# A two-layer graph network on one core: TensorE's work for three chunks set side by side, in written order

## The chip, the core and the metric

The kernel runs on one core of a Trainium2 chip. The core has five engines with a queue of instructions each: TensorE (PE; its weight loads are listed apart as PEld), VectorE (DVE), ScalarE (ACT), GpSimd (POOL) and SyncE (SP). DMA queues move data between HBM and the on-chip memories; those that fetch rows by a list of indices are issued by POOL, plain ones by SP and ACT. The metric is the time of one execution in device microseconds (us); the median of four runs is 15922.23 us (15918.34 to 15925.62).

## The reference

There are 50000 nodes with 128 features, and 850000 edges (src, dst, rel), sorted by dst, with one of 16 relations each. Two layers of this kind run one after the other, and the result is added to x and normalized:

```python
def _rgcn_layer(h, src, dst, rel, basis, w_comp, loop_w, bias):
    W = jnp.einsum('rb,bio->rio', w_comp, basis)          # 16 relations from 8 bases
    seg = dst.astype(jnp.int32) * N_REL + rel.astype(jnp.int32)
    agg = jax.ops.segment_sum(h[src], seg, num_segments=N_ENT * N_REL)
    agg = agg.reshape(N_ENT, N_REL, -1)
    msg = jnp.einsum('nri,rio->no', agg, W)
    out = msg + h @ loop_w + bias
    return jax.nn.relu(out)
...
x = _layernorm(x + layer2(layer1(x)), axis=-1)
```

## The kernel before, in words

**Chunks.** The edges are cut into runs of 672, two runs to a chunk: C = 633 chunks, the last with one run. Edges from a node to itself are taken out of the runs beforehand and handled apart ("node tiles", below), which leaves at most 640 edges a run: 5 rows of 128 (`HALF`), 10 a chunk (`K`). The function `runs(g, ...)` prepares a group of 128 runs (64 chunks): it closes up the runs on DVE (`closed_up`, six steps), turns source indices and destination keys on PE (`put`, L382 to 389; transposes at L388), writes the relations to HBM (REL), computes each run's place among the nodes (`slot`, L410 to 436), and collects the edges from a node to itself (`loops_of`, ten more steps of `closed_up`), whose relations go to LREL in HBM by one scatter of POOL per group (L491, ten in all). It is a generator; in layer one, each chunk takes one step of it for the next group (L688 to 692), beginning with the third chunk of a group. Group 0 is prepared before and during chunk 0.

**A chunk's work, in the order in which it is written.**

1. Ten gathers on POOL (L697, recorded as L187): each fetches 128 rows of h, one per edge, into one tenth of a buffer `g`. Six such buffers take turns (`GATHERS`), so a gather writes where the chunk six before it was read.
2. For every fourth chunk `weights` (L544): loads relations, compares them on DVE (`is_rel`), and five products on PE (L556) give each edge its eight basis weights in PSUM (`pm`). DVE makes `hot` (L711): for each edge, eight weights spread over 12 places for the destination nodes.
3. **Products with A** (L722): ten products g x hot in two halves of five, each half copied by ACT into `aT` (L729). A float32 product is recorded as two matmuls.
4. After the first half, `finish` for the chunk before: **products with bases** (`slots`, L619: eight products over the bases, summed in PSUM, copied by ACT), then **products with nodes** (L634 places the sums at their nodes, L638 adds what the chunk before carried over), the sum with the own part `L` (L640), and the store of 128 nodes to H1 (L647), or in layer two `normed` and the store to the output (L651).
5. Also after the first half, `from_itself` for as many node tiles of 128 nodes as are due (391 tiles over 633 chunks, six of them at chunks 0 and 1): load `h_own`, transpose on PE (L194), two products with four bases each (L599) into one PSUM buffer `hb`, weighted by DVE (L602), the loop product (L609), a sum on DVE (L612) and the store to `L`. For every eighth tile `loop_weights` (L565) loads LREL and makes the weights of the edges from a node to itself with two products (L582).
6. The loads for `finish`: `ls_of` from L and, in layer two, `xw` from x.

**What sets the order.** The program is traced in that order, and the framework's planner then orders each engine's queue by its own estimate of when things are ready; on the chip each engine runs its queue strictly in the planned order and waits on semaphores. So PE's order above is the planner's, and it may take the work of several chunks in turn. Gathers of layer two read H1 and wait for all of it. `count_up` (L499), traced in the last chunk of layer one, has one small product and tells whether the preparation held; if not, a slow path runs, which doesn't happen here.

Of the kernel before, what the change touches and what calls it, by code (L numbers as in the profile page):

```python
# [38 lines left out]
F32 = mybir.dt.float32  # L39
# [36 lines left out]
def tile_rgcn_resnorm(  # L76
# [255 lines left out]
    def runs(g, pool, asked):  # L332
# [58 lines left out]
        put(srcf, src)  # L391
# [12 lines left out]
        put(keyf, key)  # L404
        rel8 = pool.tile([P, LIVE], U8, name="rel8")
        nc.scalar.copy(rel8, quarters[:, :LIVE, 3])
        nc.sync.dma_start(REL[r0 : r0 + P], rel8)
        yield
# [15 lines left out]
        nc.scalar.copy(offs, po[:HALF, :])  # L424
        po = ps_o.tile([P, D], F32, name="po")
# [102 lines left out]
    def chunked():  # L528
        with (
# [14 lines left out]
            def weights(c, n):  # L544

                rel = hp.tile([P, LIVE], U8, name="rel")
                nc.sync.dma_start(
                    rel,
                    bass.AP(tensor=REL.tensor, offset=REL.offset + 2 * c * LIVE, ap=[[LIVE, AT], [0, NR], [1, LIVE]]),
                )  # L550
                is_rel = hp.tile([P, LIVE], F32, name="is_rel")
                nc.vector.tensor_scalar(is_rel, rel, its_rel, None, op0=OP.is_equal)  # L552
                pm = ps_m.tile([P, AT * PER * NB], F32, name="pm")
                of = pm.rearrange("e (t j) -> e t j", t=AT)
                for j in range(PER):
                    nc.tensor.matmul(  # L556
                        of[:, :, j * NB : (j + 1) * NB],
                        is_rel[:, j * P : (j + 1) * P],
                        EACH[n],
                        start=True,  # L560
                        stop=True,
                    )
                return pm.rearrange("e (t b) -> e t b", b=NB)

            def loop_weights(i, n):  # L565
# [13 lines left out]
                nc.vector.tensor_scalar(is_rel[:m], rel[:m], its_rel1[:m], None, op0=OP.is_equal)  # L579
                po = ps_o.tile([P, D], F32, name="po")  # L580
# [6 lines left out]
                return lw  # L587

            def from_itself(i, of, lw, n):

                m = min(P, N - i * P)
                h = sb.tile([P, D], F32, name="h_own")
                nc.sync.dma_start(h[:m], of[i * P : i * P + m, :])
                hT = turned(h[:m], m, sb)
                by = sb.tile([P, NB + 1, D], F32, name="by", bufs=1)
                few = BANK // D
                for b in range(0, NB, few):
                    hb = ps_h.tile([P, BANK], F32, name="hb")
# [8 lines left out]
                    )  # L607
                po = ps_o.tile([P, D], F32, name="po")
# [4 lines left out]
                nc.sync.dma_start(L[n][i * P : i * P + m, :], ls[:m])  # L613

# [11 lines left out]
            def finish(kept, c, k, aT, n0, ls, xw, n):  # L626

                st = slots(c, k, aT, n)
# [51 lines left out]
            some = ()  # L680
            for n, of in enumerate((x, H1)):
                kept, late, looked, lw = None, None, 0, None
                for c in range(C):
# [9 lines left out]
                    ks = HALF * min(2, R - 2 * c)  # L693
                    n0 = at(c)
                    g = rows[(n * C + c) % GATHERS]
                    for k in range(ks):
                        gather(g[:, k, :], of, src[:, c * K + k : c * K + k + 1])  # L697
                    if n == 0 and c == 0:
                        done(first_runs)
                    if c % Q == 0:  # L700
                        pm = weights(c, n)
                    t0 = c % Q * K
                    own = hp.tile([P, K, WN], F32, name="own")
                    nc.vector.tensor_tensor(
                        own[:, :ks],
                        grid[:, None, :WN].to_broadcast([P, ks, WN]),
                        key[:, c * K : c * K + ks, None].to_broadcast([P, ks, WN]),
                        op=OP.is_equal,
                    )
                    hot = hp.tile([P, K, NB, WN], F32, name="hot")  # L710
                    nc.vector.tensor_tensor(  # L711
                        hot[:, :ks],
                        pm[:, t0 : t0 + ks, :, None].to_broadcast([P, ks, NB, WN]),
                        own[:, :ks, None, :].to_broadcast([P, ks, NB, WN]),
                        op=OP.mult,
                    )
                    aT = hp.tile([P, NB, S], F32, name="aT")
                    for k in range(0, ks, PER):
                        m = min(PER, ks - k)
# [13 lines left out]
                        if k == 0:  # L733
                            if late is not None:
                                kept = finish(kept, *late)
                            while looked < asked(c):
                                if looked % AT == 0:
                                    lw = loop_weights(looked, n)
                                from_itself(looked, of, lw[:, looked % AT, :], n)
                                looked += 1  # L740
                    ls = sb.tile([P, D], F32, name="ls_of")
                    nc.sync.dma_start(ls, L[n][ds(n0, P), :])
                    xw = None
                    if n:
                        xw = sb.tile([P, D], F32, name="xw")
                        nc.sync.dma_start(xw, x[ds(n0, P), :])
                    late = c, ks, aT, n0, ls, xw, n
# [4 lines left out]
                finish(kept, *late)  # L752
# [188 lines left out]
```

## Time and profile before

| | |
|---|---|
| median of four runs | 15922.23 us |
| the profiled execution's own time | 15926.42 us |
| its span | 15924.6 us |
| granted clock of TensorE, mean | 0.767 |
| POOL: gathers of layer one / two | 6007.5 us / 5983.5 us busy, 6325 each |
| PE: products with A (L722) | 5592.9 us busy, 25300 matmuls |
| PE: products with bases (L619) | 3785.8 us busy, 20256 matmuls |
| PE: products with nodes (L634, L638) | 605.4 and 547.7 us busy |

A line of the timeline reads: start, length, engine, line of the kernel, operation, what it writes <- what it reads, shape, count, and in brackets how long the engine had been idle before and what ended that. A line of the groups reads: line, engine, operation, tiles, shapes, count | busy us, mean ns of one | idle us of the engine before them and what ended most of it. Busy time leaves out the fixed step between two instructions of an engine, and the time in which a gather's rows travel.

### The profile page before, as it was taken

How to read it: one execution, taken by the hardware profiler on the slowest of the kernel's cores; microseconds unless marked ns; L12 is line 12 of the kernel's file. 1: busy time of each engine (PE TensorE's matmuls, PEld its weight loads, DVE VectorE, ACT ScalarE, POOL GpSimd, SP SyncE). 2: the span in 40 equal slices, each digit the busy share in tenths (PEclk: the TensorE clock that was granted, in tenths of full speed). 3: DMA queues.
4: the chain of work that ended last, by engine and by line, in shares of the span. 5: the costliest groups of instructions: out<-in, count | busy, mean ns of one | idle time of the engine just before them, and what ended most of it. 6: DMA issues, size and time to landing. Idle time of an engine off the chain costs nothing.

```text
span 15924.6 us, 190376 instructions
## 1 busy us (share of the span) xinstructions
PE 11711.7 (74%) x59828; PEld 9645.4 (61%) x59828; DVE 6491.1 (41%) x14282; ACT 2763.7 (17%) x7931; POOL 12005.3 (75%) x12673
## 2 busy tenths in 40 slices
PE   5767677777777676767777777777777777777777
PEld 4656565656656565656666666666666666666666
DVE  5434444343434343433344444444444444444443
ACT  1111111111111111111111111111111111111111
POOL 7777777777777777777777777777777777777777
PEclk8777777777777777777777777777777777777777
DMA  3222222222222222222222222222222222222222
GB/s 84 76 72 76 72 77 72 76 72 76 72 76 72 75 72 73 72 74 73 71 76 77 78 78 78 78 78 78 78 78 78 78 78 78 77 78 78 78 77 72
DMA packets 1169578, 1207.74 MB, mean 76 GB/s; under 512 B 285749, under 2 KB 960949, under 8 KB 1168560
## 3 DMA queue, kind: packets, MB, share of 16 engines
q0 software_dynamic: 405232, 830.17, 20.2%
q1 hardware_dynamic: 760112, 363.84, 8.0%
q8 instruction: 481, 7.88, 0.2%
q14 instruction: 537, 4.40, 0.1%
q10 hardware_dynamic: 3216, 1.45, 0.0%
HBM read 1058.61 MB, written 135.71 MB: 75 GB/s over the span
## 4 chain that ended last, share of the span: by engine, by line
PE 36%; DMA 34%; issue 18%; POOL 5%; DVE 1%; ACT 0%; POOLq 0%; SPq 0%; DVEq 0%; ACTq 0%
DMA g<-H,src 18%; DMA g<-in_x_dram,src 16%; PE ps L619 15%; PE pa L722 10%; PE hb L599 6%; POOL g L187 5%; PE pm L556 2%; PE pn L634 1%; PE pn L638 1%; PE po L609 1%; PE po L194 1%; PE po L582 0%; DVE ls L612 0%; DVE hot L711 0%; DMA lrel<-LREL 0%
## 5 line engine op out<-in xcount | busy, mean ns | idle before, releaser
L722 PE MATMUL pa<-hot,g 128*128 128x96 f32 x25300 | 5592.9, 337 | 3957.1 <-DMA g<-H,src 1905.8
L722 PEld LDWEIGHTS pa<-hot,g 128*128 128x128 f32 x25300 | 4331.0, 229 | 5390.2 <-DMA g<-H,src 2354.0
L187 POOL DMA_INDIRECT g<-in_x_dram,src x6325 | 6007.5, 950 | 1952.0 <-issue 1085.3
L187 POOL DMA_INDIRECT g<-H,src x6325 | 5983.5, 946 | 1943.9 <-issue 1082.4
L619 PE MATMUL ps<-basis,aT 128*120 128x128 f32 x20256 | 3785.8, 362 | 22.3 <-ACT aT L729 22.1
L619 PEld LDWEIGHTS ps<-basis,aT 128*120 128x120 f32 x20256 | 3605.6, 266 | 102.1 <-ACT aT L729 52.2
L729 ACT COPY aT<-pa 128x480 f32<-128x480 f32 x2530 | 1414.4, 559 | 9013.0 <-PE pa L722 9000.6
L602 DVE TENSOR_TENSOR by<-hb,lw 128x512 f32<-128x512 f32 x1564 | 1079.1, 690 | 3989.2 <-PE hb L599 3964.9
L711 DVE TENSOR_TENSOR hot<-pm,own 128x960 f32<-128x960 f32 x1266 | 1445.7, 1150 | 1616.8 <-PE pa L722 1002.9
L599 PE MATMUL hb<-basis,hT 128*128 128x512 f32 x3128 | 1827.4, 669 | 10.8 <-ACT hT L196 7.9
L612 DVE TENSOR_REDUCE ls<-by 128x128 f32<-128x1152 f32 (+1 forms) x782 | 1648.6, 2108 | 2.9
L630 DVE TENSOR_SCALAR own<-fixed,slot 120x128 f32<-120x128 f32 x1266 | 433.5, 342 | 1097.5 <-PE pn L634 1095.5
L623 ACT COPY slots<-ps 120x128 f32<-120x128 f32 x1266 | 337.8, 267 | 2436.6 <-PE ps L619 2434.5
L634 PE MATMUL pn<-slots,own 120*128 120x128 f32 x2532 | 605.4, 326 | 19.5 <-ACT slots L623 16.9
L640 DVE TENSOR_TENSOR a<-pn,ls_of 128x128 f32<-128x128 f32 x1266 | 358.5, 283 | 617.5 <-DMA ls_of<-L 192.9
L634 PEld LDWEIGHTS pn<-slots,own 120*128 120x128 f32 x2532 | 479.2, 226 | 207.4 <-issue 85.8
L599 PEld LDWEIGHTS hb<-basis,hT 128*128 128x128 f32 x3128 | 540.8, 216 | 17.2 <-ACT hT L196 12.7
L638 PE MATMUL pn<-kept,shift 128*128 128x128 f32 x2528 | 547.7, 302 | 0.0
L643 ACT COPY kept<-pn 128x128 f32<-128x128 f32 x1264 | 340.6, 269 | 1075.1 <-DVE a L640 1056.3
L556 PEld LDWEIGHTS pm<-each,is_rel 128*128 128x128 f32 x3180 | 450.4, 213 | 86.8 <-issue 77.8
L521 DVE RECIPROCAL rs<-sd 128x1 f32<-128x1 f32 x633 | 100.8, 159 | 941.5 <-ACT sd L519 938.6
L556 PE MATMUL pm<-each,is_rel 128*128 128x64 f32 x3180 | 455.6, 292 | 8.7 <-DVE is_rel L552 8.7
(142 smaller groups left out, 4989.2 us busy)
## 6 DMA issues: line engine op xcount, KB each, us to landing
g<-in_x_dram,src POOLq DMA_INDIRECT x6325
g<-H,src POOLq DMA_INDIRECT x6325
ls_of<-L SPq DMA_DIRECT2D x1266, 64.0 KB
L<-ls SPq DMA_DIRECT2D x780, 64.0 KB
H<-h SPq DMA_DIRECT2D x633, 64.0 KB
xw<-in_x_dram SPq DMA_DIRECT2D x633, 64.0 KB
out_dram<-o SPq DMA_DIRECT2D x633, 64.0 KB
rel<-REL SPq DMA_DIRECT2D x318, 80.0 KB
```

Source lines behind the costliest of these rows:

```text
L187: nc.gpsimd.indirect_dma_start(out=to, out_offset=None, in_=of, in_offset=bass.IndirectOffsetOnAxis(ap=idx, axis=0))
L556: nc.tensor.matmul(of[:, :, j * NB : (j + 1) * NB], is_rel[:, j * P : (j + 1) * P], EACH[n], start=True, stop=True,)
L599: nc.tensor.matmul(hb[:m], hT, BASIS[n][:, b : b + few, :].rearrange("p b d -> p (b d)"), start=True, stop=True)
L602: nc.vector.tensor_tensor(by[:m, b : b + few, :], hb[:m].rearrange("p (b d) -> p b d", d=D), lw[:m, b : b + few, None].to_broadcast([m, fe ...
L612: nc.vector.tensor_reduce(ls[:m], by[:m].rearrange("p b d -> p d b"), AX.X, OP.add)
L619: nc.tensor.matmul(ps[: k * WN], aT[:, b, : k * WN], BASIS[n][:, b, :], start=b == 0, stop=b == NB - 1)
L630: nc.vector.tensor_scalar(own[: k * WN], grid[: k * WN, :P], slot[: k * WN, c : c + 1], None, op0=OP.is_equal)
L634: nc.tensor.matmul(pn, own[: k * WN], st[: k * WN], start=True, stop=not c)
L638: nc.tensor.matmul(pn, shift, kept, start=False, stop=True)
L711: nc.vector.tensor_tensor(hot[:, :ks], pm[:, t0 : t0 + ks, :, None].to_broadcast([P, ks, NB, WN]), own[:, :ks, None, :].to_broadcast([P, k ...
L722: nc.tensor.matmul(pa[:, i * NB * WN : (i + 1) * NB * WN], g[:, k + i, :], hot[:, k + i].rearrange("e b w -> e (b w)"), start=True, stop=True,
L729: nc.scalar.copy(aT[:, :, k * WN : (k + m) * WN].rearrange("d b (i w) -> d i b w", w=WN), pa[:, : m * NB * WN].rearrange("d (i b w) -> d i ...
```

## The change

PE's instructions in the two layers are put under a manual schedule: PE's queue takes them exactly as they are traced. The other engines stay with the planner. The tracing is rearranged so that one iteration holds, for PE, in this order:

- nodes for chunk c-2 (`nodes_of`, the second part of the old `finish`);
- the weights and the transpose of the first node tile of this iteration;
- A, first half, for chunk c;
- that tile's first basis product, then bases for chunk c-1 (`slots`), then the tile's second basis product;
- A, second half, for chunk c;
- the rest of that tile (the loop product), and all further node tiles of this iteration, each from its beginning to its end;
- weights for the chunk after, if it is the first of four.

`weights`, `loop_weights` and `from_itself` become generators, so that their loads and DVE's comparisons are traced an iteration ahead of their products, and `hot` of the next chunk at the end of an iteration. The node tiles of chunks 0 and 1 all come at chunk 1. `ls_of` and `xw` are loaded an iteration after their chunk's A products, for nodes an iteration later. `runs` gets three more pauses; for all groups but the first the transposes of the source indices move behind one of them, so all later steps of a group, its scatter too, are traced two chunks later.

```diff
-        put(srcf, src)
+        if g == 0:
+            put(srcf, src)
...
-        put(keyf, key)
         rel8 = pool.tile([P, LIVE], U8, name="rel8")
         nc.scalar.copy(rel8, quarters[:, :LIVE, 3])
         nc.sync.dma_start(REL[r0 : r0 + P], rel8)
+        yield
+        if g:
+            put(srcf, src)
+        put(keyf, key)
         yield
...
         nc.scalar.copy(offs, po[:HALF, :])
+        yield
...
-            def from_itself(i, of, lw, n):
+            def from_itself(i, of, n, lws):
 
                 m = min(P, N - i * P)
+                if i % AT == 0:
+                    weigh = loop_weights(i, n)
+                    next(weigh)
                 h = sb.tile([P, D], F32, name="h_own")
                 nc.sync.dma_start(h[:m], of[i * P : i * P + m, :])
+                yield
+                if i % AT == 0:
+                    lws[:] = [next(weigh)]
+                lw = lws[0][:, i % AT, :]
                 hT = turned(h[:m], m, sb)
...
                 for b in range(0, NB, few):
+                    yield
                     hb = ps_h.tile([P, BANK], F32, name="hb")
...
+                yield
                 po = ps_o.tile([P, D], F32, name="po")
                 nc.tensor.matmul(po[:m], hT, LOOP[n], start=True, stop=True)
...
-            def finish(kept, c, k, aT, n0, ls, xw, n):
-
-                st = slots(c, k, aT, n)
+            def nodes_of(kept, c, k, st, n0, ls, xw, n):
+
...
+            ordered = ExitStack()
+            ordered.enter_context(tc.manual_schedule(engines={mybir.EngineType.PE}))
             for n, of in enumerate((x, H1)):
...
+                def own_nodes(c):
+
+                    return range(asked(c - 1) if c > 1 else 0, asked(c) if c else 0)
...
                 for c in range(C):
...
+                    if c == 0:
+                        if n == 0:
+                            done(first_runs)
+                        pm = next(weigh)
+                        hot = hot_of(c, pm)
+                    if c > 1:
+                        kept = nodes_of(kept, c - 2, ks(c - 2), summed_up, base[2], *others, n)
+                        others = loaded(base[1])
+                    parts = own_parts[0] if own_parts else iter(())
+                    next(parts, None)
...
                         if k == 0:
-                            if late is not None:
-                                kept = finish(kept, *late)
-                            while looked < asked(c):
-                                if looked % AT == 0:
-                                    lw = loop_weights(looked, n)
-                                from_itself(looked, of, lw[:, looked % AT, :], n)
-                                looked += 1
...
+                            next(parts, None)
+                            if c:
+                                summed_up = slots(c - 1, ks(c - 1), multiplied, n)
+                            next(parts, None)
+                    multiplied = aT
+                    for parts in own_parts:
+                        done(parts)
+                    if c == 1:
+                        others = loaded(base[1])
+                    if c + 1 < C:
+                        if (c + 1) % Q == 0:
+                            pm = next(weigh)
+                        hot = hot_of(c + 1, pm)
+                        if c + 2 < C and (c + 2) % Q == 0:
+                            weigh = weights(c + 2, n)
+                            next(weigh)
+                        own_parts = []
+                        for i in own_nodes(c + 1):
+                            own_parts.append(from_itself(i, of, n, lws))
+                            if len(own_parts) == 1:
+                                next(own_parts[0])
...
-                finish(kept, *late)
+                last = loaded(base[0])
+                kept = nodes_of(kept, C - 2, ks(C - 2), summed_up, base[1], *others, n)
+                summed_up = slots(C - 1, ks(C - 1), multiplied, n)
+                nodes_of(kept, C - 1, ks(C - 1), summed_up, base[0], *last, n)
+            ordered.close()
```

## The prediction

> **What bounds the kernel now.** I read the page's busy shares first, then its groups, then the waits of POOL alone, then stretches of PE, then the timeline around the two kinds of place where PE falls behind.
>
> ```profile
> PE 11711.7 (74%) x59828; PEld 9645.4 (61%) x59828; DVE 6491.1 (41%) x14282; ACT 2763.7 (17%) x7931; POOL 12005.3 (75%) x12673
> ...
> PE 36%; DMA 34%; issue 18%; POOL 5%; DVE 1%; ACT 0%; POOLq 0%; SPq 0%; DVEq 0%; ACTq 0%
> ...
> L187 POOL DMA_INDIRECT g<-in_x_dram,src x6325 | 6007.5, 950 | 1952.0 <-issue 1085.3
> L187 POOL DMA_INDIRECT g<-H,src x6325 | 5983.5, 946 | 1943.9 <-issue 1082.4
> ```
>
> POOL and PE look level (75% and 74%), and the chain runs mostly along PE and the gathers' landings. But POOL's gathers are 6007.5 + 5983.5 us busy and 1952.0 + 1943.9 us idle before them: 15886.9 of the 15924.6 us of the span. POOL's waits say what the idle time is (columns: total, times, longest, in us):
>
> ```profile
> POOL g L187 <- issue: 2167.7, 7112, 0.3
> POOL g L187 <- PE pa L722: 597.4, 1960, 0.3
> ...
> POOL g L187 <- ACT src L389: 24.6, 1, 24.6
> POOL g L187 <- DMA H<-h: 16.4, 1, 16.4
> ```
>
> Whatever a wait is put down to, it lasts 0.3 us: that is the fixed step between two gathers. Only two are longer: 24.6 us until the first indices exist, 16.4 us between the layers. So POOL never waits for a buffer, and a gather costs (15886.9 - 24.6 - 16.4) / 12650 = 1.253 us, a chunk of ten 12.5 us. PE has far more room (columns: length, PE busy, granted clock, DMA share, GB/s):
>
> ```profile
> 74.50:115.70 41.20, 3.07 (x19) 0.57 0.21 57
> 115.70:119.50 3.80, 3.76 (x14) 0.50 0.48 126
> 123.30:200.00 76.70, 69.94 (x464) 0.98 0.36 98
> 1143.90:1198.80 54.90, 2.67 (x19) 0.57 0.22 56
> 1198.80:1240.10 41.30, 41.25 (x311) 0.95 0.38 107
> ```
>
> In the last stretch PE catches up without a pause: 311 matmuls in 41.3 us, 0.133 us each. A chunk has 59828 / 1266 = 47.3, so 6.3 us against POOL's 12.5. The first and fourth stretch show PE standing 41 and 55 us, and POOL does not feel it, since six gather buffers let it run 75 us ahead. Only what exhausts that lead, or lies ahead of the first or behind the last gather of a layer, can cost time.
>
> **The change part by part.** The profiled run took 15926.4 us for a span of 15924.6; that is 4.2 above the median of 15922.2. I add my sum to the median.
>
> *Steady state: 0.* The matmuls, copies and DMAs of a chunk are the same; the bases' 16 products and copy (L619, L623) move one iteration behind A, the nodes' products (L634, L638), their DVE and ACT steps and the store to H1 or out another. SP's loads move too: h_own, lrel and rel are issued an iteration before their use, ls_of and xw for the chunk behind. A written order can stall PE, e.g. at the second basis product, which shares one PSUM buffer with the first and waits for DVE's 0.69 us (L602); the bases' 1.93 us stand between them. What hides any such stall is POOL's 12.5 us against 6.3; without that cover each us per chunk would cost 1266 us. Nothing is queued on POOL but gathers and ten scatters.
>
> *put, moved a step later, and three new pauses: 0.* The transposes (L388, two groups of five, 1.33 us each) come ten chunks into a group of 64, their indices are due some 48 chunks later. For the first group the indices' half is not moved, so the first gather stays at 28.2 us.
>
> *The start of layer one: +18 us.* The loops' scatter stands on POOL behind the first 60 gathers:
>
> ```profile
> 109.53 1.00 POOL L491 DMA_INDIRECT LREL<-l_rel,l_to  x1 [0.30 <-issue]
> 115.74 1.11 PE L582 MATMUL po<-each,is_l 128*128 128x64 f32 x4 [38.16 <-DVE is_l L579]
> 134.07 0.27 PE L194 MATMUL po<-ident,h_own 128*128 128x128 f32 x1
> 139.62 0.27 PE L194 MATMUL po<-ident,h_own 128*128 128x128 f32 x1
> 144.96 0.27 PE L194 MATMUL po<-ident,h_own 128*128 128x128 f32 x1
> 150.17 0.27 PE L194 MATMUL po<-ident,h_own 128*128 128x128 f32 x1
> ...
> 136.78 0.94 POOL L187 DMA_INDIRECT g<-in_x_dram,src  x1 [0.30 <-PE hb L599]
> ```
>
> Before, half of chunk 1's A products ran ahead of this wait, and those of chunk 2 between the node tiles' own products. Written out, tile 0's weights (L582) and transpose stand ahead of chunk 1's A products, and all six node tiles asked for there ahead of chunk 2's; all of PE's later work queues behind that wait, and POOL behind the A products. From 116.9 us (115.74 + 1.11): transpose 0.42 and its start, 0.3; five A products at the granted clock of 0.50 (second row of the stretches) 2.2 (30 matmuls took 6.69 at 70 us); basis 1.9; bases 1.9; basis 1.05; five A products 1.25; loop 0.4: 126.3. Five more tiles in a row: the rows show one per 5.4 us ((150.17 - 134.07) / 3), DVE alone taking 0.69 + 0.68 + 0.28 + 2.13 = 3.8: 153.3. Nodes of chunk 0 and half of chunk 2's A products, 1.7: 155.0. The gather that refills chunk 2's buffer now starts at 136.78 (line above). Late by 18. Ends: 10 with DVE's 3.8 us per tile, 31 with 8 us (two tiles with a weights step between them stand 9.4 apart, 155.99 to 165.35); a gain is excluded, for POOL does not wait here now. I take 18, nearest to rows of the same tiles. After it PE gains 6 us a chunk.
>
> *The other nine scatters: +10 us.* Each holds DVE, then PE:
>
> ```profile
> 1192.05 1.00 POOL L491 DMA_INDIRECT LREL<-l_rel,l_to  x1 [0.30 <-DMA g<-in_x_dram,src]
> 1194.28 0.16 DVE L480 SCALAR_TENSOR_TENSOR l_to<-odd,d_i 128x1 int32<-128x1 f32 x1 [59.48 <-DMA LREL<-l_rel,l_to]
> 1198.81 2.45 PE L722 MATMUL pa<-hot,g 128*128 128x96 f32 x10 [52.23 <-DVE hot L711]
> ```
>
> PE stood with two chunks more done than POOL needed, so POOL had 2 x 12.5 + 1.3 us left after the scatter began, and PE had half a chunk done 9.2 us after it (1201.26): 17 us to spare. In written order PE stops sooner: the second half of a chunk's A products stands behind a basis product that needs DVE. With 1 chunk done 4.6 us are left; with half a chunk 1.7 are missing; with none 8. I weigh these 0.35 (two chunks), 0.35, 0.2 and 0.1: 1.1 us each, 10 in all. Ends: 0 and 9 x 8 = 72.
>
> *Between the layers and at the end: +4.* After a layer's last A product half of the bases of the chunk before is left now (8 matmuls, 1.96 us at 7980.56, 1.76 at 15907.38); written out all 16 are (3.67 at 7985.00 and 15910.65): 1.7 and 1.9, and count_up's product ahead of them in layer one, 0.4. Ends: 0 (part of it beside ACT's copies) and 8.
>
> *POOL's pace: 0.* The gathers' mean of 950 and 946 ns stands above the 0.94 us of the usual row; in the first 50 us, beside dense DVE work, single ones take up to 2.89 (44.15 us). DVE's work stays the same. Ends: a gain of (10 + 6) ns x 6325 = 101 us if all of this went, a loss of the same size.
>
> Sum: 18 + 10 + 4 = 32; 15922.2 + 32 = 15954, rounded up to 15955.
>
> **Two rules of the Trainium skill.** Perfetto Trace Analysis, section Identifying the Most-Contended Engine, has the engine of highest occupancy optimized first, and PE judged by its weight loads; by that POOL (75%) stands over PE (61%), and a change on PE gains nothing. That speaks against this change; by it alone the time is 15922. For the gathers' long rows, SBUF — State Buffer, section Who interferes with whom, lets a DVE instruction in a two-port mode block GpSimd for its whole length; by it the 101 us depend on when DVE runs, and the time could reach 15821.
>
> **The rivals.** (1) *Not slower: the lead holds.* If the six tiles' work ends before POOL wants chunk 2's buffer, the start costs nothing. It decides at 136.8 us: the tiles would need (136.8 - 126.3 - 1.7) / 5 = 1.8 us each, or the scatter a place some 15 gathers earlier. For it: before, POOL got through a 52 us pause of PE nine times. Against: DVE's 3.8 us per tile. Price: only the ends, 15926, with some events 15936. (2) *The scatters cost more.* If PE stops right at the scatter's chunk and the refill runs slowly, each costs 8 to 20 us: 9 x 14 + 22 = 148, 16070. For it: PE's order can no longer pass DVE's. Against: six buffers, and PE's 6.3 us. (3) *PE becomes the bound*: stalls of over 6.2 us in each chunk; one us beyond is 1266 us, 17200. No row shows a stall of that size within a chunk. (4) *Faster*, if the gathers' excess shrinks: a third of 101 less 22, 15910; half of it needed to pass 0.2%.
>
> **How the numbers follow.** Forecast (+20 to +60: 15942 to 15982) 0.55; (1) 0.18; (2) 0.20; (3) 0.03; (4) 0.04. What a measurement of this kernel tells from no change is taken as 0.2%, 32 us; the forecast lies on that line, a little less than half of it (0.24) under. Slower: 0.31 + 0.20 + 0.03 = 0.54; same: 0.24 + 0.18 = 0.42; faster 0.04. The range reaches down to 15918, through (1), and up to 16090, through most of (2); (3) and the far ends stay out.
>
> **What would show it.** Right: POOL's waits of 0.3 us everywhere, the first gather at 28, the layers' gap at 17 to 20, and one new wait of POOL for PE's A products of 10 to 31 us near 137. Short ones behind the other scatters show that step. Wrong: no such wait (1), waits over 8 us after each scatter (2), POOL waiting in layer two (3), or gathers' means moved by over 3 ns.

## The result and the profile after

| | before | after |
|---|---|---|
| median | 15921.8 us (15916.78 to 15927.14) | 15950.45 us (15946.03 to 15957.35) |
| ratio, with its 95% interval | | 1.0018 (1.0013 to 1.0023) |
| span of the profiled execution | 15924.6 us | 15949.4 us |

The change costs 28.65 us, 0.18%: surely more than nothing, and just under the 0.2% that was set as the line. The forecast was 15955. The page of the kernel after, engines and gathers:

```profile
PE 11913.7 (75%) x59828; PEld 9725.5 (61%) x59828; DVE 6564.9 (41%) x14282; ACT 2828.5 (18%) x7931; POOL 12007.8 (75%) x12673
...
L187 POOL DMA_INDIRECT g<-in_x_dram,src x6325 | 6001.7, 949 | 1978.1 <-issue 1058.9
L187 POOL DMA_INDIRECT g<-H,src x6325 | 5991.9, 947 | 1940.9 <-issue 1050.5
```

Nothing has changed in kind: the gathers, with the idle time before them, still fill 15912.6 of 15949.4 us. So the difference must be somewhere on POOL, and its waits (us in total, times, longest) show one that was not there:

```profile
POOL g L187 <- issue: 2109.4, 6921, 0.3
POOL g L187 <- PE pa L768: 668.3, 2107, 26.3
...
POOL g L187 <- ACT src L389: 24.5, 1, 24.5
POOL g L187 <- DMA H<-h: 13.5, 1, 13.5
```

Before, the longest wait for PE's products with A was 0.3 us; now one is 26.3. POOL's timeline has it at the 81st gather, the first that refills chunk 2's buffer (start, length, ..., in brackets the idle time before and what ended it):

```profile
132.96 0.94 POOL L187 DMA_INDIRECT g<-in_x_dram,src  x1 [0.30 <-issue]
160.22 0.94 POOL L187 DMA_INDIRECT g<-in_x_dram,src  x1 [26.31 <-PE pa L768]
```

The account of the two spans, each term the difference of rows above from those of before: the new wait +26.0 (26.3 less the step of 0.3 that every gather has); the gathers' busy time in layer one -5.8, in layer two +8.4; the gap between the layers 13.5 for 16.4, -2.9; from the last gather's end to the end of the span 18.94 for 19.65, -0.7. Sum 25.0, against 24.8 us between the spans. The medians lie 28.65 apart; single executions of either kernel spread over 10 us.

**Why 26 us.** PE's timeline behind the first scatter:

```profile
114.28 1.11 PE L589 MATMUL po<-each,is_l 128*128 128x64 f32 x4 [41.00 <-DVE is_l L585]
115.70 0.48 PE L194 MATMUL po<-ident,h_own 128*128 128x128 f32 x1 [0.30 <-ACT lw L593]
...
124.71 0.41 PE L625 MATMUL po<-loop,hT 128*128 128x128 f32 x2
125.50 0.33 PE L194 MATMUL po<-ident,h_own 128*128 128x128 f32 x1 [0.38 <-DVE by L626]
...
129.50 2.07 PE L614 MATMUL hb<-basis,hT 128*128 128x512 f32 x2 [2.19 <-DVE by L617]
...
132.56 0.47 PE L194 MATMUL po<-ident,h_own 128*128 128x128 f32 x1 [0.55 <-DVE by L626]
...
139.30 0.48 PE L194 MATMUL po<-ident,h_own 128*128 128x128 f32 x1 [0.56 <-DVE by L626]
...
146.10 0.48 PE L194 MATMUL po<-ident,h_own 128*128 128x128 f32 x1 [0.56 <-DVE by L626]
...
152.90 0.48 PE L194 MATMUL po<-ident,h_own 128*128 128x128 f32 x1 [0.56 <-DVE by L626]
...
159.37 0.80 PE L768 MATMUL pa<-hot,g 128*128 128x96 f32 x4
```

The weights of tile 0 (L589) come when the scatter allows, and one tile and chunk 1's products with A are through at 125.1 us. Then come five tiles in a row, 6.8 us each, and only behind the last of them chunk 2's products with A, for which POOL has been waiting since 133.9. In the kernel before such tiles stood 5.4 us apart, with other chunks' products between them. The stretch of the five tiles (length, PE busy and its instructions, granted clock, DMA share, GB/s) says what is different:

```profile
125.50:159.00 33.50, 24.02 (x36) 0.55 0.13 35
...
125.50:129.00 3.50, 1.46 (x3) 1.00 0.31 75
129.20:159.00 29.80, 22.56 (x33) 0.50 0.11 31
```

PE stops for DVE or ACT before three of a tile's four steps, with pauses of 0.35 to 2.2 us, and its granted clock falls to 0.50 at about 129 us and stays there, where the stretch shown of before (123.30 to 200.00) had 0.98. A pair of basis products with 512 columns takes 2.07 us here and 1.02 at 122.76; PE's own instructions for one tile add up to 5.3 us (0.48 + 2.08 + 2.07 + 0.63 from 139.30 on). The page "TensorE: Matmul & The Clock Gate" of the Trainium skill, section "A second HAM failure mode: psum-queue depth-cycling", tells of frequent short idle times of PE between groups that make its clock go down and up. The fall here agrees with it; a rise between the tiles isn't seen before the stretch ends. The clock isn't all of it, either: in the kernel with eight tiles (experiment 1) the first of the tiles in a row had its pairs in 1.13 and 1.12 us, at a clock of 0.95, and still took 6.1 us (123.15 to 129.25), with one wait of 2.18 us for DVE.

**The tiles alone cost nothing.** Layer two has the same five tiles in a row behind chunk 1, 6.1 to 6.8 us each (8039.33 to 8071.77), but no scatter ahead of them. There chunk 2's products with A begin at 8072.20, 39 us before the gather that needs their buffer is due:

```profile
8072.20 2.29 PE L768 MATMUL pa<-hot,g 128*128 128x96 f32 x10
...
8111.05 0.94 POOL L187 DMA_INDIRECT g<-H,src  x1 [0.30 <-PE pn L654]
```

So it takes both here, the tiles in a row and a lead that the scatter has used up.

**The ends became shorter.** Behind the last product with A of layer one, before:

```profile
7982.30 1.81 PE L556 MATMUL pm<-each,is_rel 128*128 128x64 f32 x8
...
7985.00 3.67 PE L619 MATMUL ps<-basis,aT 128*60 128x128 f32 x16
```

and after:

```profile
8000.41 3.51 PE L636 MATMUL ps<-basis,aT 128*120 128x128 f32 x16
8003.86 0.19 PE L509 MATMUL po<-pick,ones 128*1 128x2 f32 x2
...
8004.92 1.96 PE L636 MATMUL ps<-basis,aT 128*60 128x128 f32 x16
...
8007.97 1.23 PE L562 MATMUL pm<-each,is_rel 128*128 128x64 f32 x10
```

As forecast, all 16 base products are left (3.51 us; before 8 in 1.96). But the 16 behind them, the last chunk's own, now take 1.96 us where they took 3.67 at 7985.00 before: the granted clock in their stretch is 1.00 (8004.20 to 8008.00), before 0.51 (7985.00 to 7988.70). Why it is up there isn't shown: before, too, PE had worked without a pause ahead of them, for 5 us (7980.02 to 7985.00), at a clock of 0.50. And one thing is gone from this place: the planner had put eight of the ten matmuls for layer two's first weights (L556), 1.81 us, ahead of the last chunk's; in written order all ten stand behind the last nodes' products (L562, 8007.97). From the first of these base products to the last chunk's nodes' products it is 6.8 us now (8000.41 to 8007.23), 8.6 before (7980.56 to 7989.20). At the end of layer two the base products do the same (3.44 us for 1.76, then 1.96 for 3.67), without weights between them.

**The other nine scatters cost nothing,** though each holds PE longer. The pause of 52 us at 1146 us of the kernel before is now:

```profile
1234.01 2.24 PE L768 MATMUL pa<-hot,g 128*128 128x96 f32 x9 [66.05 <-DVE hot L718]
```

POOL has no wait over 0.3 us behind any of them. How near it came, by the times of the records: the shortest time from the end of a product with A to the gather that refills its place was 11.6 to 20.7 us behind the nine scatters before, and is 2.7 to 13.8 us now (2.7 behind the fifth of the ten).

### The profile page after: what moved, and what is told of

Same layout as the page of the kernel before. It is cut to its first block, busy times and chain, and to the rows that moved or that the text cites. A ratio compares the mean times of both kernels' runs of the same rounds, so it can differ in the third digit from the quotient of the medians.

```text
span 15949.4 us, 189416 instructions
## 1 busy us (share of the span) xinstructions
PE 11913.7 (75%) x59828; PEld 9725.5 (61%) x59828; DVE 6564.9 (41%) x14282; ACT 2828.5 (18%) x7931; POOL 12007.8 (75%) x12673
## 4 chain that ended last, share of the span: by engine, by line
PE 38%; DMA 30%; issue 17%; POOL 5%; DVE 3%; ACT 0%; POOLq 0%; SPq 0%; DVEq 0%; ACTq 0%
DMA g<-H,src 16%; DMA g<-in_x_dram,src 13%; PE ps L636 13%; PE pa L768 12%; PE hb L614 10%; POOL g L187 5%; DVE hot L718 2%; DVE ls L628 1%; PE pm L562 1%; PE po L625 1%; PE pn L650 1%; PE pn L654 1%; PE po L194 0%; DVE by L626 0%; PE po L589 0%
## 5 line engine op out<-in xcount | busy, mean ns | idle before, releaser
L768 PE MATMUL pa<-hot,g 128*128 128x96 f32 x25300 | 5191.4, 333 | 3409.5 <-DMA g<-H,src 1517.6
L768 PEld LDWEIGHTS pa<-hot,g 128*128 128x128 f32 x25300 | 4191.7, 229 | 4737.8 <-DMA g<-H,src 1931.1
L636 PEld LDWEIGHTS ps<-basis,aT 128*120 128x120 f32 x20256 | 3865.3, 280 | 765.0 <-issue 764.7
L614 PE MATMUL hb<-basis,hT 128*128 128x512 f32 x3128 | 2289.5, 824 | 71.7 <-DVE by L617 66.8
L614 PEld LDWEIGHTS hb<-basis,hT 128*128 128x128 f32 x3128 | 666.9, 263 | 89.3 <-DVE by L617 81.5
L650 PE MATMUL pn<-slots,own 120*128 120x128 f32 x2532 | 541.3, 297 | 10.0 <-ACT kept L659 5.3
L194 PE MATMUL po<-ident,h_own 128*128 128x128 f32 (+1 forms) x782 | 246.7, 315 | 381.8 <-DVE by L626 345.2
L653 DVE TENSOR_SCALAR shift<-fixed,dist 128x128 f32<-128x128 f32 x1264 | 425.8, 337 | 0.2
L562 PE MATMUL pm<-each,is_rel 128*128 128x64 f32 x3180 | 417.7, 281 | 0.0
L650 PEld LDWEIGHTS pn<-slots,own 120*128 120x128 f32 x2532 | 402.3, 200 | 12.2 <-ACT kept L659 5.6
L654 PEld LDWEIGHTS pn<-kept,shift 128*128 128x128 f32 x2528 | 404.4, 201 | 2.3 <-DVE shift L653 2.1
```

Source lines behind the costliest of these rows:

```text
L562: nc.tensor.matmul(of[:, :, j * NB : (j + 1) * NB], is_rel[:, j * P : (j + 1) * P], EACH[n], start=True, stop=True,)
L614: nc.tensor.matmul(hb[:m], hT, BASIS[n][:, b : b + few, :].rearrange("p b d -> p (b d)"), start=True, stop=True)
L636: nc.tensor.matmul(ps[: k * WN], aT[:, b, : k * WN], BASIS[n][:, b, :], start=b == 0, stop=b == NB - 1)
L650: nc.tensor.matmul(pn, own[: k * WN], st[: k * WN], start=True, stop=not c)
L654: nc.tensor.matmul(pn, shift, kept, start=False, stop=True)
L768: nc.tensor.matmul(pa[:, i * NB * WN : (i + 1) * NB * WN], g[:, k + i, :], hot[:, k + i].rearrange("e b w -> e (b w)"), start=True, stop=True,
```

## The experiments

The theory: the 26 us are the node tiles that the written order puts ahead of chunk 2's products with A, less the lead that POOL still has there; everything else is small. Rivals: what matters is the scatter's place on POOL, the number of buffers, or the amount of work in any order; and the gathers' own pace takes part.

The experiments fell on two chips. On the first, where the kernel before takes 15920.56 us, four kernels were run once each beside one run of before, so differences of less than some 10 us say nothing. On the second the kernel before takes 19245.8 us in one comparison and 19270.68 in the other, 21% more. Eight runs were made there, two of them of one kernel (5); the kernel after itself was not run. What that chip does differently is told first, since it limits what those eight can say.

**The second chip.** A thousand us in the middle of layer one (length, POOL busy and its instructions, granted clock, DMA share, GB/s), of the kernel after on a chip like the first:

```profile
3000.00:4000.00 1000.00, 756.45 (x799) 0.75 0.27 74
```

and of the kernel with spread tiles (below) on the second:

```profile
3000.00:4000.00 1000.00, 637.89 (x672) 0.73 0.24 62
```

POOL's instruction takes as long as ever (756.45 / 799 = 0.947 us, 637.89 / 672 = 0.949), but it issues 672 in place of 799. By the records' times, a gather's rows are read by PE in the median 2.8 us after its issue has ended on the one, and 81.3 us on the other. That uses up the six buffers: 0.9 (issue) + 81.3 + 0.3 (product) + 6.1 (from the product to the refill) = 88.6 us for 60 gathers, 1.48 us each, 14.8 us a chunk. So POOL waits there all along:

```profile
POOL g L187 <- issue: 2870.9, 9171, 4.6
POOL g L187 <- PE pa L768: 1631.1, 1369, 8.9
POOL g L187 <- remote: 1621.7, 1225, 7.9
```

("remote" is a releaser that the profile doesn't name.) It doesn't look as if the rows came late: by the DMA records the packets of the gathers' queue keep up with the issues on both chips (at 3000 us 2001 gathers were issued on the second, and packets for as many had ended; 2340 on the first), and PE's waits that are put down to rows of gathers are 12 us in all there, against 2728 in the kernel after. PE comes to the rows late. Why isn't settled; the profile names few of the releasers there. Where every buffer is waited for, a step that holds one longer should cost time in every chunk, and one that frees it sooner should gain it; the times there can't be carried to the first chip. What can be compared are the single events at the start.

**1. Two tiles fewer or more ahead of chunk 2's products with A.** `AHEAD` says how many node tiles are asked for in advance; the kernel after has six at chunks 0 and 1, this gives four and eight.

```diff
-AHEAD = 4
+AHEAD = 2
```

> The changed kernel with node tiles asked for two ahead (four tiles at chunk 1), once more, for a chip on which the kernel before runs at its usual 15922 us. Theory: POOL's long wait 26.3 - 2 x 6.8 = 12.7 us, time about 15937. Rival (the scatter's late place alone): 26 us, 15950.

> The changed kernel with node tiles asked for six ahead (eight tiles at chunk 1), once more, for the same reason. Theory: POOL's long wait 39.9 us, time about 15964. Rival: 26 us, 15950.

Measured on the first chip: 15934.68 us with four tiles, 15966.14 with eight. POOL's timeline of the kernel with four:

```profile
145.76 0.94 POOL L187 DMA_INDIRECT g<-in_x_dram,src  x1 [12.21 <-PE pa L768]
```

and with eight:

```profile
170.51 0.94 POOL L187 DMA_INDIRECT g<-in_x_dram,src  x1 [36.46 <-PE pa L768]
```

The same one gather waits 12.2, 26.3 and 36.5 us, and the times follow: 15934.7, 15950.5, 15966.1. In the kernel with four the transposes stand at 124.79, 131.84 and 138.58, 6.7 to 7.1 us apart, and in the one with eight from 136.00 on at 6.8: that is the price of a tile. (With eight, chunk 1's second half of products with A ran 2.4 us sooner, at 121.27 for 123.62, so its wait is 36.5 and not 40.)

The same two on the second chip:

> The changed kernel with node tiles asked for two ahead instead of four, so that four tiles instead of six come at chunk 1. Theory: POOL's long wait is a fixed part plus 6.8 us for each tile (transposes of the changed kernel at 132.56 to 152.90, three steps): 26.3 - 13.6 = 12.7 us, time about 15937. Rival (the wait is the scatter's late place alone, whatever the tiles): 26 us, 15950.

> The changed kernel with node tiles asked for six ahead, so eight at chunk 1. Theory: POOL's long wait grows by 2 x 6.8 us to 39.9 us, time about 15964. Rival (the scatter's place alone): 26 us, 15950.

Measured: 18884.8 us, ratio 0.9812 (0.9796 to 0.9829), and 18944.46 us (one run). With four tiles:

```profile
162.22 0.94 POOL L187 DMA_INDIRECT g<-in_x_dram,src  x1 [17.33 <-PE pa L768]
```

with eight:

```profile
189.28 0.94 POOL L187 DMA_INDIRECT g<-in_x_dram,src  x1 [44.69 <-PE pa L768]
```

The expected times had the first chip in view and don't apply. The wait is there, at the same gather, and 27.4 us for four tiles is 6.8 a tile again. On that chip layer two has such a wait as well, at its own 81st gather; with four tiles and with eight:

```profile
9596.62 0.94 POOL L187 DMA_INDIRECT g<-H,src  x1 [19.71 <-PE pa L768]
...
9662.92 0.94 POOL L187 DMA_INDIRECT g<-H,src  x1 [47.01 <-PE pa L768]
```

It is 34.6 us with six (experiment 6) and 7.0 with two (experiment 4): the place of the tiles once more.

**2. The scatter ahead of the gathers.** From chunk 4 on, the gathers of layer one are made to follow the scatter that was traced last, so POOL issues each scatter when the program comes to it and not 60 gathers in.

```diff
+    scattered = {}
...
-        nc.gpsimd.indirect_dma_start(
+        scattered[g] = nc.gpsimd.indirect_dma_start(
...
-                    for k in range(ks(c)):
-                        gather(g[:, k, :], of, src[:, c * K + k : c * K + k + 1])
+                    with ExitStack() as behind:
+                        if n == 0 and c >= 4:
+                            behind.enter_context(tc.issue_after(scattered[max(scattered)].ins))
+                        for k in range(ks(c)):
+                            gather(g[:, k, :], of, src[:, c * K + k : c * K + k + 1])
```

> The changed kernel with layer one's gathers from chunk 4 on behind the last scatter, once more, for the same reason. Theory: the first scatter at about 80 us, POOL's long wait 0 to 3 us, time 15922 to 15928; PE's pauses at the other scatters 20 to 45 us instead of 65, which moves no time. Rival (six tiles in a row cost whenever they come): 26 us, 15950. On a chip where gathers land slowly, the early scatter made the kernel slower than its siblings, for POOL waits for DVE there.

Measured on the first chip: 15927.99 us. The scatter and the gather that waited before:

```profile
82.26 1.00 POOL L498 DMA_INDIRECT LREL<-l_rel,l_to  x1 [0.30 <-issue]
...
134.11 0.95 POOL L187 DMA_INDIRECT g<-in_x_dram,src  x1 [0.30 <-PE pa L773]
```

The scatter goes at 82 us in place of 108, tile 0 and chunk 1's products with A start 26 us sooner (90 for 116), chunk 2's products with A begin at 133.06, and the wait is gone: just so, for the shortest time from product to refill is 0.5 us here. This is the undoing of the lead's loss, with all tiles in their place and written order kept, and it takes back 22 of the 28.65 us; of the spans of the profiled executions, 23.3 of the 24.8 us (15926.1 for 15949.4 after and 15924.6 before). The edit moves the other nine scatters too, behind which no wait stood. What is left is less than one run can tell; layer two's gathers have 5992.5 us busy, as after, and 9 above before.

> The changed kernel with layer one's gathers from chunk 4 on queued behind the last loops' scatter traced so far, so that POOL issues the first scatter after 40 gathers, at about 80 us, instead of after 60, at 107.6; the others come two to four chunks earlier. Theory (the wait is the scatter's arrival plus six tiles in a row, against a buffer due at 134): PE starts 27 us earlier, the wait of 26.3 us shrinks to 0 to 3, time 15922 to 15928; PE's pauses at the other nine scatters shrink from about 65 us to 20 to 45 without moving the time. Rival (six tiles in a row cost whenever they come): 26 us stay, 15950.

On the second chip: 19094.5 us, ratio 0.9923 (0.9906 to 0.9939), and the theory fails there: the scatter goes at 82.33 us, but the wait stays. The gather, and the group of the scatter in that run:

```profile
174.45 0.95 POOL L187 DMA_INDIRECT g<-in_x_dram,src  x1 [31.08 <-PE pa L773]
...
L498 POOL DMA_INDIRECT LREL<-l_rel,l_to x10 | 11.3, 1130 | 214.0 <-DVE own L648 120.1 <-DVE l_rel L483 93.6 <-issue 0.3
```

The wait of 31.1 us is that of experiment 6's kernel there (shown in 4), whose scatter goes at 106.45. In both PE gets to the first tile's second basis product only at 134 us (134.71 and 133.76), and the other five tiles follow in a row. So something later than the scatter holds the start on that chip. The profile doesn't name it: PE waits for DVE, and DVE until 133.96 for "remote". And the edit does harm: nine of the ten scatters stand on POOL 19 to 28 us before DVE has the list ready, and all gathers queue behind them: 214 us. On the first chip the group's idle time was 3.0 us in all. An order forced on POOL's queue holds only while the others keep their pace.

**3. A seventh buffer.**

```diff
-GATHERS = 6
+GATHERS = 7
```

> The changed kernel with seven gather buffers instead of six. Theory of the lead (a buffer more gives POOL 12.5 us more before it needs chunk 2's buffer): the long wait shrinks from 26.3 to about 14 us, time 15938. Rival (the planner sets the first scatter where the buffers are full, then after 70 gathers instead of 60, so that PE starts 12.5 us later): the wait stays at 26 us, time 15950.

Measured on the first chip: 15952.8 us, the rival's. POOL's timeline:

```profile
119.19 1.00 POOL L496 DMA_INDIRECT LREL<-l_rel,l_to  x1 [0.30 <-issue]
...
169.30 0.94 POOL L187 DMA_INDIRECT g<-in_x_dram,src  x1 [24.06 <-PE pa L768]
```

The scatter now stands behind 70 gathers, not 60: the planner fills every buffer it has before it. Everything behind it moves some 11.6 us later, and so does the wait, now at the 91st gather. More buffers lengthen the lead and the delay alike, so the theory's forecast for this run was wrong; what counts is the time from the scatter to the refill, against the tiles that stand between.

**4. Two tiles a chunk.** The tiles of the start are spread over the first chunks.

```diff
-                    return range(asked(c - 1) if c > 1 else 0, asked(c) if c else 0)
+                    return range(min(asked(c - 1), 2 * (c - 1)) if c > 1 else 0, min(asked(c), 2 * c) if c else 0)
```

> The kernel after with at most two node tiles in a chunk's turn at the start, in place of four in chunk 1's; nothing else moves, and the order on TensorE stays written. Theory: the products of chunk 2 stand behind two tiles fewer, some 14 us at 6.8 us a tile, and those of chunk 3 behind two more, with 12.5 us more time; GpSimd's wait falls from 26 to between 0 and 14 us in all, time 15924 to 15938 us. Rival (TensorE is held by something other than the tiles, such as the late weights of tile 0 at 114 us): the wait stays at 20 us or more, time 15945 us or more.

The expectation miscounts: six tiles are written in chunk 1's turn in the kernel after, so four are moved, not two. Measured on the second chip: 18871.4 us, ratio 0.9791 (0.9775 to 0.9808). POOL's timeline:

```profile
148.99 0.94 POOL L187 DMA_INDIRECT g<-in_x_dram,src  x1 [4.20 <-PE pa L768]
...
185.76 0.94 POOL L187 DMA_INDIRECT g<-in_x_dram,src  x1 [8.86 <-PE pa L768]
```

The neighbour for comparison is the kernel of experiment 6, which has all six tiles there, on the same chip and in the same comparison:

```profile
173.50 0.94 POOL L189 DMA_INDIRECT g<-in_x_dram,src  x1 [31.07 <-PE pa L772]
```

31.1 us become 4.2 at the gather in question and 8.9 at a later one: 26.9 us less at the first, four tiles of 6.7. That the place of the tiles makes the wait is shown here too; that this is worth some 25 us on the first chip wasn't run.

**5. TensorE's order given back to the planner.** The chunks stay side by side, only the schedule is not the written one.

```diff
-            ordered.enter_context(tc.manual_schedule(engines={mybir.EngineType.PE}))
```

> The changed kernel without the manual schedule: the tracing is the changed one, but the planner orders PE again. Theory (the written order holds chunk 2's A products behind six node tiles in a row): the planner takes A products between the tiles, so POOL's one long wait for them (26.3 us in the changed kernel) is gone or under 3 us, and the time is 15920 to 15926. Rival (the new tracing, with all six tiles at chunk 1 and the later scatters, costs by itself): a wait of 10 us or more stays, 15935 to 15950. The gap between the layers, 13.5 us in the changed kernel, should go back to about 16.

> The kernel after with one thing undone: TensorE's order is no longer the written one, the scheduler places the instructions again; the three side-by-side chunks stay. Theory (the 26 us wait at the start comes from four node tiles that stand in the written order before the products of chunk 2): the scheduler can put the products of chunk 2 ahead of the tiles' products, GpSimd's wait at gather 80 goes, and the time is 15920 to 15928 us; the gap between the layers goes back from 13.5 to about 16 us, since the 16 base products at the end are no longer in a row. Rival (the wait belongs to the amount of work at the start, whatever its order): the wait stays at 20 us or more and the time is 15945 us or more.

Measured on the second chip, in both comparisons: 19003.54 us, ratio 0.9874 (0.9858 to 0.9891), and 19013.92 us, 0.9862 (0.9843 to 0.9882). The times of the expectations don't apply there. The start, in the second of them:

```profile
140.03 0.95 POOL L187 DMA_INDIRECT g<-in_x_dram,src  x1 [11.10 <-PE pa L767]
...
231.91 0.94 POOL L187 DMA_INDIRECT g<-in_x_dram,src  x1 [11.04 <-PE pa L767]
```

The wait of 31 us for chunk 2 is gone, for smaller ones at several gathers (11.1 at the 76th, 4.9 at the 121st, 11.0 at the 131st); those are partly that chip's own (experiment 4's kernel waits 5.1 at the 76th). So the long wait does belong to the written order; but waits of over 10 us are left, which the first expectation had given to its rival. The gap between the layers is 40 us in both runs, 35 to 42 in the others on that chip, and says nothing about the 16 us. Whether the planner's order of this program would be level with before on the first chip stays open.

**6. The comparison `is_rel` in another form.** The same values, but with a second tensor operand that lies in PSUM, a form in which DVE takes 0.87 us for 0.55 (rows below).

```diff
+    tile16 = consts.tile([P, 1], F32, name="tile16")
...
+        nc.vector.tensor_scalar(tile16, its_tile, float(NR), None, op0=OP.mult)
...
-                nc.vector.tensor_scalar(is_rel, rel, its_rel, None, op0=OP.is_equal)
+                nc.vector.scalar_tensor_tensor(
+                    is_rel, rel, tile16, apart[:, 0:1].to_broadcast([P, LIVE]), op0=OP.add, op1=OP.is_equal
+                )
```

> The kernel after with one VectorE operation in another form: the comparison of line 557 is made with two tensor operands, one of them in PSUM, in place of one tensor and a scalar; the value is the same. Theory (the gathers' excess over 0.94 us, 56 us in layer one and 46 in layer two, comes in good part from this comparison, which stands beside the gathers and holds back GpSimd's descriptor writes): the gathers' busy time falls by 8 to 11 us in each layer, time 15930 to 15942 us, wait at gather 80 unchanged at 26 us. Rival (the excess comes from elsewhere, or is only moved): busy times within 3 us of 6001.7 and 5991.9, time 15948 to 15955 us.

This is about the 8.4 us that layer two's gathers lost. A pair of the kernel after, DVE's comparison and the gather beside it:

```profile
9736.48 0.55 DVE L557 TENSOR_SCALAR is_rel<-rel,its_rel 128x640 f32<-128x640 uint8 x1
9736.59 1.26 POOL L187 DMA_INDIRECT g<-H,src  x1 [0.30 <-DMA g<-H,src]
```

and of the kernel with the other form:

```profile
9739.06 0.96 POOL L189 DMA_INDIRECT g<-H,src  x1 [0.31 <-issue]
9739.11 0.87 DVE L559 SCALAR_TENSOR_TENSOR is_rel<-rel,tile,fixed 128x640 f32<-128x640 uint8 x1
```

Over all gathers of layer two that overlap the comparison: before 221 with a mean of 1.000 us, after 226 with 1.019, against 0.944 and 0.945 for the rest; with the other form 221 with 0.944, and 0.944 for the rest. So in the mean the slower comparison (0.87 us for 0.55) holds up no gather. The chip isn't the reason: in experiment 4's kernel, with the quick form on the same chip, 158 gathers of layer two overlap it, with a mean of 1.000, and the rest have 0.944. That agrees with the section "Who interferes with whom" of the Trainium skill's "SBUF — State Buffer", which the prediction drew on, as far as one form holds up gathers and the other doesn't; whether the quick form blocks for its whole length, as the section has it, isn't shown (the gather above gained 0.32 us, and the two overlap for 0.44). The quick form's size is 12.3 us in layer two before (221 x 0.056) and 16.7 after (226 x 0.074): 4.4 of the 8.4 us that were lost. Why a gather beside it loses more in the new order isn't shown. Measured on the second chip: 18892.36 us, ratio 0.9805 (0.9788 to 0.9822), with these gathers:

```profile
L189 POOL DMA_INDIRECT g<-H,src x6325 | 5969.2, 944 | 3465.6 <-issue 1454.3
L189 POOL DMA_INDIRECT g<-in_x_dram,src x6325 | 5987.1, 947 | 3399.7 <-issue 1433.2
```

In the kernel of experiment 4, beside it, they are 5978.6 and 5997.9: 9.4 and 10.8 more, in the theory's range; but that kernel differs in its tiles too, and the planner's kernel shows that two executions of one program can differ by 7 to 9, so these sums alone show little. The whole time gains nothing from it there, since POOL waits for buffers. The wait at the 81st gather is there unchanged (31.07, shown above).

**7. Three edits together:** 2, 4 and 6.

> The kernel after with three edits together: the scatter of each group's list is issued before the gathers that follow chunk 3, at most two node tiles in a chunk's turn at the start, and the comparison of line 557 in the form with two tensor operands. Theory: no wait of GpSimd over 1 us after the first scatter (15926 us), and 16 to 22 us less in the gathers, so 15904 to 15910 us, below both kernels. Rival (the gathers' excess does not come from the comparison): 15922 to 15928 us, level with the kernel before.

Measured on the second chip: 19050.43 us, ratio 0.989 (0.9873 to 0.9906), slower than experiment 4 alone by 179 us. The early scatter does here what it did in 2: its group is idle 211.4 us. At the start waits of 4.5 us (81st gather) and 6.9 (101st) are left, where the theory had none over 1. The forecast below both kernels was for the first chip and wasn't tried there.

No run shows a version that beats both kernels where the kernel before takes 15920 us. On the second chip every relative of the kernel after beat the kernel before, by 0.8 to 2.1%; the two nearest to it (1 with four tiles, 6) by 1.9 and 2.0%. So the change, too, would probably gain there, but neither it nor the reason was run.

## Why the prediction was right or wrong

**What bounds the kernel: right.** The gathers, back to back at a step of 0.3 us. PE's busy time rose by 202 us and the time by 29; what counts is where POOL's lead ends.

**The start of layer one: right in place and mechanism, +26.0 for 18.** The forecast named the gather (near 137 us; it was due at 134.2), the wait (for chunk 2's products with A) and the reason, and put chunk 1's end at 126.3 us (125.1). The term that failed is "one per 5.4 us": five tiles took 33.9 us, 6.8 each. The 5.4 was taken from a stretch where the planner had set other chunks' products between the tiles and PE had a clock of 0.98; with only tiles in the queue it has 0.55. The end with 8 us a tile, at 31, held it. Experiments 1 and 4 show that the wait follows the number of tiles, 2, on the first chip, that it follows the scatter's time. That the low clock lengthens a tile is read from the rows; no run changed the clock alone, and the one tile in a row that ran at 0.95 (experiment 1, with eight) took 6.1 us, not 5.4.

**The other nine scatters: 0 for +10.** The weights given to "half a chunk done" and "none" (0.3 together) were too high: POOL's margin, 11.6 to 20.7 us before, is 2.7 to 6.0 behind five of the nine, about the case "one chunk" (4.6), and 11.7 to 13.8 behind the others. 2.7 us at the worst is not much: the forecast's mechanism is there, and stops short of costing anything.

**Between the layers and at the end: -3.6 for +4, wrong in sign.** All 16 base products are left, as the step has it. What it had wrong: it left the last chunk's 16 at their 3.67 us, and they took 1.96 at a clock of 1.00; and it didn't count that matmuls for the weights (1.81 us), which stood ahead of the last chunk's before, come behind them in written order.

**POOL's pace: +2.6 net for 0.** Within the bounds of 101 us either way; experiment 6 shows one cause and the size of its part.

**Steady state and `put`: 0, as forecast.** No gather but the one waits.

**The sum:** 32 forecast, 28.65 measured, with 8 us too little at the start, 2.6 in the gathers not foreseen, and 17.6 too much at the scatters and the ends. That these nearly cancel is luck: the total is better than its terms. The forecast also gave "slower" by its own line of 32 us more weight (0.54) than "same" (0.42), and the time came out 3 us under that line. **The rivals:** (1), the lead holds, is what experiment 2 makes of it; in the kernel after the tiles would have had to take 1.8 us each. (2), scatters that cost 8 to 20 us each, (3) and (4) didn't happen. The rule of "Perfetto Trace Analysis" on the engine of highest occupancy, which gave 15922, was right that such a change gains nothing, but had no place for the loss: work on PE, which is not the bound, still cost 26 us, through one buffer at one moment.

## What to carry to other kernels

When an order of instructions is written out in place of a planner's, look first at the places where the engine stands still for something outside, and write there what the bounding engine needs before what is merely due: four tiles more or less ahead of one product are 24 to 27 us, and nothing else in two times 633 chunks cost as much. A duration taken from a row carries the clock of its surroundings, so where the change alters what stands beside an operation, price it from a row with like surroundings or take the slow end. A margin that costs nothing on one chip can be used up all along on another, so a forced order across queues should be tried on more than one.

## What was not expected of the hardware

- One of the two chips took 21% longer for the same kernel, with a POOL instruction of the same length (0.949 us), packets that move as soon as they are issued, and PE reading the rows 81 us after their issue in place of 2.8.
- PE's granted clock decides single steps in both directions: the same 16 base products took 1.96 us at 1.00 and 3.67 at 0.51; the pair of 512-column products 2.07 us at 0.50, between pauses of 0.35 to 2.2 us, and 1.02 at 1.00.
- A comparison on DVE that takes 0.32 us longer, with a second operand in PSUM, takes nothing from the gathers in the mean, where the quick form lengthens those beside it by 0.06 to 0.07 us in the mean and by up to 0.3 in single ones of layer two.
